# A two-layer graph network on one core: where in a group of matmuls the pieces of layer 1 are run

## The chip, the cores and the metric

The kernel runs on one core of a Trainium2 chip. The metric is the device time of one execution in microseconds (us); the time given for a kernel is the median of its runs. The engines are called TensorE (PE in the profile), VectorE (DVE), ScalarE (ACT), GpSimd (POOL) and SyncE (SP), which issues most DMAs.

## The reference

There are 4096 nodes with 512 features, and a 0/1 adjacency matrix of 4096 x 4096. Layer 0 is graph attention with 8 heads of 64 features, layer 1 is attention inside 32 graphs of 128 nodes. Each is added to its input and normalized by row.

```python
# layer 0
feats = jnp.einsum('nf,hfo->hno', X, W)
dense = s_self[:, :, None] + s_neigh[:, None, :]
dense = jnp.where(dense > 0, dense, 0.2 * dense) * A[None]
out = jnp.einsum('hij,hjo->hio', softmax(dense), feats) + b[:, None, :]
x = layernorm(x + relu(concat_heads(out)))
# layer 1
query, key, value = x @ Wq.T + bq, x @ Wk.T + bk, x @ Wv.T + bv
a = where(same_graph, query @ key.T / sqrt(512), 0.0)
scores = (a + adj + adj) * where(same_graph, 1.0, -1e6)
x = layernorm(x + (softmax(scores) * same_graph) @ value)
```

## The kernel before, in words

**Layer 0** is streamed over the adjacency (`adjacency_streamed_path`). There are four passes, one for each pair of heads (`main_pass(r)`, r = 0 to 3). A pass has four chunks of 1024 target rows (`c` = 0 to 3), and a chunk sums over 32 tiles of 128 source rows. In the last pass they go four at a time, so a chunk has eight groups, numbered 0 to 7 here. For each source tile and head VectorE makes one tile q (L1348, 128 x 1024), and a mark is made of it by ScalarE (L1357), or for every eighth by VectorE (L1353). There are six buffers for q in the last pass, and a group needs eight. TensorE makes three sums: accf, the products of the adjacency with the features f ("A f", L1368, 16 matmuls in a group); acc, the products of the features g with q (L1388, 64 matmuls in the trace); and dens, the products with the marks (L1402), after every second group (the odd ones). After each group ScalarE also checks one or two blocks of the adjacency (L1128, L1129).

**The last pass also carries layer 1.** When a chunk is done, its sums are turned to rows and the rows enter layer 1 in two blocks of 512, called a and b. The work is cut into pieces, which generators run one at a time:

- E (`sums_to_rows`): sums of the chunk that just ended to rows. TensorE transposes into PSUM (L1199, L1222), VectorE reads that (L1202, L1223). E also starts the rows of layer 0 of block a (`rows_of_layer_0`: loads of x and of hp_l on SP's queue, L1144 on VectorE, and the statistics of the normalization, L524 and L525, and L527 and L528 on GpSimd).
- R: the same rows for block b. F: the last part of such a normalization, four operations L532 on VectorE.
- a and b, each in nine steps (`layer_1`, cut by its `yield`s). Steps 1 and 2: each eight transposes L954 and two copies L955 to x1T on ScalarE. Steps 3 and 4: each 16 products L974, to zT by L981 on ScalarE; step 3 has also four L988 on VectorE. Step 5: 32 products L1001 and the softmax (L1010, L1026 and others). Step 6: values of two tiles (2 x 8 products L1046, VectorE's L1054 for each) and between them four transposes L1075. Step 7: the output rows of these two tiles (L1060, L1062, a normalization, the stores). Step 8: values of the two other tiles. Step 9: their output rows.

Block b of a chunk isn't finished in it: its steps 6 to 9 run in the next chunk. So each of chunks 1 to 3 carries a and b of the chunk before it, and chunks 2 and 3 the rest of an older b too; in chunk 1 there is none, and such pieces do nothing.

**What sets the order.** TensorE's instructions run in the order of the program (`tc.manual_schedule(engines={PE})`); the order on the other engines is made by the compiler's planner from program order and the times that it expects. Within a group the program has: the eight q and their marks, accf, two loads of adjacency tiles, the pieces of the *first place* (L1382), acc, the pieces of the *second place* (L1395), dens, the other loads, the checks. `PLAN` and `PLANS` (L1256, L1257) say by letter which pieces go to which place: eight pairs for the eight groups, (first place, second place), the last pair or two different in chunk 3. The PSUM tiles of all pieces come from `misc` (L552), which hands out three banks in turn; so a tile must wait for the readers of the tile three before it. After the last chunk, what is left is run in a fixed order (L1456).

Of the kernel before, what the change touches and what calls it, by code (L numbers as in the profile page):

```python
# [404 lines left out]
def adjacency_streamed_path(  # L405
# [847 lines left out]

    PLAN = [("E", "Fb"), ("b", "b"), ("b", "a"), ("Ra", "Fa"), ("a", "b"), ("ba", "b")]  # L1256
    PLANS = PLAN + [("ab", ""), ("aaba", "")], PLAN + [("a", ""), ("aa", "a")]  # L1257
    plan = {"b": None}

    def run_plan(todo):  # L1260
        for k in todo:
            if k == "F":
                plan[k]()
                continue
            gen = ends[0] if k == "E" else plan[k]
            if gen is not None:
                next(gen)
            if k == "E":
                ends.pop(0)
# [17 lines left out]
    def main_pass(r, ae=None, wide=4):  # L1287

        for c in range(NCH):
# [10 lines left out]
            def pieces(c, group, place):  # L1300
                if r == PR - 1 and c:
                    run_plan(PLANS[c == NCH - 1][group][place])
                elif place == (r == 0):
# [155 lines left out]
@with_exitstack  # L1459
def tile_gat_then_graph_attention(ctx: ExitStack, tc: tile.TileContext, *args: bass.AP):  # L1460
    nc = tc.nc
    keep = ctx.enter_context(tc.tile_pool(name="flag", bufs=1))
    flag = keep.tile([1, 1], I32, name="flag")
    adjacency_streamed_path(tc, flag, *args)
    other = nc.values_load(flag[0:1, 0:1], min_val=0, max_val=1)
    with tc.If(other > 0):
        general_path(tc, *args)
# [42 lines left out]
```

## Time and profile before

| What | us |
|---|---|
| median of 3 runs | 2091.82 |
| lowest and highest of them | 2089.79, 2091.85 |
| the profiled execution, whole | 2089.37 |
| its span in the profile | 2087.0 |
| chunk 1 of the last pass (about) | 158.6 |
| chunk 2 | 172.4 |
| chunk 3 | 162.2 |
| after the last chunk | 120.8 |

The span is read from the trace's start; the chunks of the last pass lie at 1473.0, 1631.6 and 1804.0 us, and the tail starts at 1966.2 us. A line of a page or of waits names engine, tile and line of the code, what it waited for, and then total us, how often and the longest. A line of a timeline has the start, the time taken, engine, line, operation, tiles and how many were merged, and in brackets the idle time before it and what ended that.

### The profile page before, as it was taken

The numbers are of one execution on the slowest core, as the hardware profiler recorded it, in microseconds if no ns is written. First come the engines' busy times: TensorE is split into PE (matmuls) and PEld (weight loads), VectorE is DVE, ScalarE is ACT, GpSimd is POOL, SyncE is SP. The second block draws the span as 40 slices with busy tenths as digits, with TensorE's granted clock in tenths as the row PEclk, the third lists the DMA queues.
The fourth block names the chain that finished last, engine by engine and source line by source line (L and its number), as shares of the span: only waits on it lengthen the run. The fifth ranks groups of instructions, "written<-read, shape, count | busy, mean of one in ns | idle before, by whom it ended". The sixth has DMA issues, their size and how long they took to land. (4 is left out here: it accounts for less than half of the span.)

```text
span 2087.0 us, 38127 instructions
## 1 busy us (share of the span) xinstructions
PE 2055.3 (98%) x15014; PEld 1011.8 (48%) x15014; DVE 1659.8 (80%) x2037; ACT 1537.4 (74%) x1819; POOL 251.0 (12%) x393
## 2 busy tenths in 40 slices
PE   8999999999999999999999999999999999999997
PEld 4556555555545444444445444544454444445443
DVE  5556887888798998797999999998975884886654
ACT  3328898888878899787899899998775666567420
POOL 2343222222100000000000000000300210210111
PEclk9999999999999999999999999999999999999999
DMA  8999999999899999897999899989964773775211
GB/s 253 266 258 242 272 292 257 301 255 298 267 334 331 363 335 342 257 312 254 334 310 339 304 350 329 324 290 360 305 238 145 240 255 126 227 272 165 73 48 43
DMA packets 207881, 551.28 MB, mean 264 GB/s; under 512 B 25292, under 2 KB 66252, under 8 KB 207692
## 3 DMA queue, kind: packets, MB, share of 16 engines
q1 hardware_dynamic: 140748, 425.79, 59.0%
q0 software_dynamic: 62784, 121.91, 23.3%
q8 instruction: 120, 1.97, 0.4%
q10 hardware_dynamic: 4160, 1.05, 0.2%
q14 instruction: 69, 0.57, 0.1%
HBM read 491.79 MB, written 107.22 MB: 287 GB/s over the span
## 5 line engine op out<-in xcount | busy, mean ns | idle before, releaser
L1348 DVE SCALAR_TENSOR_TENSOR q<-p_row,d_all,at 128x1024 f32<-128x1024 f32 x1024 | 1242.5, 1278 | 170.2 <-PE acc L1388 142.0
L1357 ACT ACTIVATE mark<-q,nb_all 128x1024 fp8e4<-128x1024 f32 x896 | 995.8, 1145 | 191.4 <-DVE q L1348 175.3
L1388 PE MATMUL acc<-q,g_s 128*32 128x512 f32 x8192 | 908.3, 594 | 3.2 <-DVE q L1348 2.9
L1388 PEld LDWEIGHTS acc<-q,g_s 128*32 128x32 f32 x8192 | 265.4, 110 | 601.3 <-issue 534.2
L1368 PE MATMUL accf<-at,f_s 128*128 128x512 f32 x2048 | 494.2, 397 | 1.9 <-issue 1.8
L1368 PEld LDWEIGHTS accf<-at,f_s 128*128 128x128 f32 x2048 | 379.8, 189 | 111.0 <-issue 29.1
L1128 ACT ACTIVATE ck<-ck,neg_half_f 128x1024 f32<-128x1024 f32 x128 | 146.0, 1141 | 21.1 <-DMA ck<-in_adj_dram 21.0
L1129 ACT ACTIVATE ck<-ck,neg_quarter 128x1024 f32<-128x1024 f32 x128 | 146.4, 1143 | 1.8
L1113 ACT CAST at<-ps_m 128x1024 fp32r<-128x1024 fp8e4 x128 | 120.2, 1026 | 10.9 <-issue 5.9
L1402 PE MATMUL dens<-mark,e_b 128*6 128x512 fp8e4 x2048 | 124.6, 379 | 0.0
L719 PE MATMUL ps_set<-w_sb_f,xT_f 128*128 128x512 f32 x256 | 116.0, 601 | 0.0
L974 PE MATMUL ps_m<-x1T,M_sb 128*128 128x512 f32 x256 | 113.1, 595 | 1.2 <-ACT x1T L955 1.2
L1046 PE MATMUL ps_m<-wvT,x1T 128*128 128x512 f32 x256 | 114.2, 594 | 0.0
L1233 POOL DMA_DIRECT2D hs_d<-hst x12 | 10.7, 894 | 841.9 <-DVE hst L1223 641.3
L1353 DVE TENSOR_SCALAR mark<-q,d_all 128x1024 fp8e4<-128x1024 f32 x128 | 95.8, 749 | 4.8
L1402 PEld LDWEIGHTS <-e_b 128*6 128x6 bf16 x2048 | 52.5, 86 | 79.4 <-issue 35.3
L1114 POOL DMA_DIRECT2D at_d<-at x128 | 68.7, 537 | 167.8 <-ACT at L1113 108.1
L741 ACT ACTIVATE fst<-fb 128x512 fp32r<-128x512 f32 x32 | 20.4, 637 | 86.1 <-DVE fb L727 52.1
L974 PEld LDWEIGHTS ps_m<-x1T,M_sb 128*128 128x128 f32 x256 | 47.9, 190 | 62.7 <-issue 59.9
L1046 PEld LDWEIGHTS ps_m<-wvT,x1T 128*128 128x128 f32 x256 | 47.6, 190 | 57.2 <-issue 56.0
L719 PEld LDWEIGHTS ps_set<-w_sb_f,xT_f 128*128 128x128 f32 x256 | 48.9, 198 | 49.5 <-issue 49.1
L1054 DVE TENSOR_TENSOR v_t<-ps_m,bv_row 128x512 f32<-128x512 f32 x32 | 21.9, 684 | 62.2 <-PE ps_m L1046 62.2
(177 smaller groups left out, 1136.6 us busy)
## 6 DMA issues: line engine op xcount, KB each, us to landing
at<-at_d SPq DMA_DIRECT2D x384, 512.0 KB, 6.0
ck<-in_adj_dram SPq DMA_DIRECT2D x128, 512.0 KB, 5.4
f_s<-f_d SPq DMA_DIRECT2D x128, 512.0 KB, 7.5
at_d<-at POOLq DMA_DIRECT2D x128, 512.0 KB, 14.7
g_s<-g_d SPq DMA_DIRECT2D x128, 256.0 KB, 5.7
f_d<-fst POOLq DMA_DIRECT2D x32, 512.0 KB, 7.7
p_row<-pu_d SPq DMA_DIRECT2D x32, 512.0 KB, 6.8
a_b<-in_adj_dram POOLq DMA_DIRECT2D x32, 512.0 KB, 16.3
```

Source lines behind the costliest of these rows:

```text
L719: nc.tensor.matmul(pf, tile_j(xTs[k][:, c].rearrange("p u n -> p (u n)"), u), w_sb[:, c, :], start=(c == 0), stop=(c == FC - 1),)
L974: nc.tensor.matmul(pz, L1["M"][:, f, ts(c, P)], x1T[:, f, :], start=(f == 0), stop=(f == FC - 1),)
L1046: nc.tensor.matmul(pv, x1T[:, f, ts(u, P)], L1["wvT"][:, f, :], start=(f == 0), stop=(f == FC - 1),)
L1113: nc.scalar.copy(at, both[:, :, k])
L1128: tc.keep_in_program_order(nc.scalar.activation(ck, ck, AF.Square, bias=neg_half))
L1129: nc.scalar.activation(ck, ck, AF.Abs, bias=neg_quarter, accum_out=binp[:, k : k + 1])
L1348: nc.vector.scalar_tensor_tensor(q, p_row[h], d_j, ats[r, c, j].bitcast(F32), op0=OP.max, op1=OP.mult)
L1353: nc.vector.tensor_scalar(mark, q, d_j, None, op0=OP.is_gt, saturate=False)
L1357: nc.scalar.activation(mark, q, AF.Sigmoid, bias=nb_all[:, j, hh : hh + 1], scale=BIG, saturate=False,)
L1368: nc.tensor.matmul(accf[:, s, :], f_s[j // 4][:, j % 4, w, :], ats[r, c, j][:, ts(s, HB)], start=(j == 0 and w == 0), stop=(j == NT - 1 an ...
L1388: nc.tensor.matmul(acc[o : o + 32, s, :], g_s[j // 4][:, j % 4, h, o % FH : o % FH + 32], qs[j, h][:, ts(s, HB)], start=(j == 0), stop=(j ...
L1402: nc.tensor.matmul(dens[lo : lo + 6, :], e_b[:, j, 2 * r + h, :], marks[j, h][:, ts(s, HB)], start=(j == 0), stop=(j == NT - 1),)
```

## The change

All pieces that stood in the second place of a group are moved to a first place, and the second places are left empty. F moves to the next group; the other pieces stay in their group. Each of a and b keeps the order of its own steps.

```diff
-    PLAN = [("E", "Fb"), ("b", "b"), ("b", "a"), ("Ra", "Fa"), ("a", "b"), ("ba", "b")]
-    PLANS = PLAN + [("ab", ""), ("aaba", "")], PLAN + [("a", ""), ("aa", "a")]
+    PLAN = [("Eb", ""), ("bFb", ""), ("ba", ""), ("Raa", ""), ("Fab", ""), ("bab", "")]
+    PLANS = PLAN + [("ab", ""), ("aaba", "")], PLAN + [("a", ""), ("aaa", "")]
```

Group by group, with the step numbers: group 0 has E and step 6 of the older b ahead of acc (before: step 6 and F behind it); group 1 step 7, F, step 8 (before: F in group 0, and step 8 behind acc); group 2 step 9 and step 1 of a (before: step 1 behind); group 3 R and steps 2 and 3 of a (before: F and step 3 behind); group 4 F, step 4 of a and step 1 of the new b (before: step 1 behind); group 5 step 2 of b, step 5 of a, step 3 of b (before: step 3 behind). Groups 6 and 7 are as before, except in chunk 3, where step 9 of a moves ahead of acc in group 7.

## The prediction

> **What bounds the kernel now.** I read the page first, for which engine is full; then the busy time by chunk of the last pass, because the change acts only there; then the waits of TensorE in that stretch; and then the timelines of the engines around each step that moves.
>
> ```profile
> PE 2055.3 (98%) x15014; PEld 1011.8 (48%) x15014; DVE 1659.8 (80%) x2037; ACT 1537.4 (74%) x1819; POOL 251.0 (12%) x393
> ```
>
> TensorE is full; the others have room on average. In the table by stretch (TensorE, weight loads, VectorE, ScalarE, GpSimd, granted clock, DMA share, GB/s), these are chunks 2 and 3 of the last pass:
>
> ```profile
> 1631.60:1804.00 172.40, 172.04 (x1033) 82.31 (x1029) 128.21 (x197) 110.17 (x148) 23.06 (x37) 1.00 0.63 211
> 1804.00:1966.20 162.20, 161.84 (x984) 75.42 (x980) 125.72 (x183) 103.31 (x132) 18.26 (x29) 1.00 0.53 178
> ```
>
> TensorE has no hole; VectorE is at about 75%. So a TensorE wait added here is paid in full: nothing later has slack to give it back. Of waits that the profile names on TensorE from 1473 to 1964 us, there are only these:
>
> ```profile
> PE acc L1388 <- DVE q L1348: 2.9, 3, 2.5
> PE ps_m L974 <- ACT x1T L955: 0.5, 1, 0.5
> ```
>
> [...] I also took each run of one line's matmuls from its first start to the start of the next run. Undisturbed, a group's 16 products L1368 take 3.8 us and its 64 products L1388 take 6.9 to 7.0. Four kinds of L1388 runs are longer: 12.0 us in group 1 of chunk 1 (5.1 lost), 8.6 and 8.0 in groups 0 and 1 of chunks 2 and 3 (1.6 and 1.0), and 7.5 to 7.8 in group 3 (0.5, 0.5, 0.8). With 0.3 in one L1368 run of chunks 2 and 3, that is 5.9 us in chunk 1 and 3.4 in each of the others: 12.7 us which waits for VectorE's q cost now. The largest, in TensorE's timeline (start, us):
>
> ```profile
> 1489.52 2.68 PE L1388 MATMUL acc<-q,g_s 128*32 128x512 f32 x16
> 1494.66 7.46 PE L1388 MATMUL acc<-q,g_s 128*32 128x512 f32 x46 [2.46 <-DVE q L1348]
> ```
>
> [...] copies L955 below start when the mark ahead of them ends. [...] here an L974 matmul is shown as 592 ns but the next starts 429 ns later, so I use starts. [...]
>
> **The change part by part.** No arithmetic is added. A step moves from behind a group's L1388 to ahead of it. Between two L1388 runs lie the second place of the one group and the first place of the next, so what moves is filler, from one such gap to the gap before; and what was cut by 7 us of L1388 now stands back to back.
>
> *F of the first block* (four L532, VectorE) goes from group 0 to group 1, behind the eight q of group 1. In chunk 1 VectorE idles 1.26 us for GpSimd's rstd and spends 1.9 on F at 1490.2 to 1493.3, with q 3 to 8 queued behind. Without that, q at 1.2 us each from 1490.2 give q8 at 1497.5 and the run ends at 1498.8, not 1501.5: **-2.7**. F then lies before the q of group 2, of which some five (four are enough) are made by the time they are needed. In chunks 2 and 3 no q waits for F.
>
> *Step 6 of b behind E, group 0 of chunks 2 and 3.* All step tiles take turns in three PSUM banks. E uses three (one L1199, two L1222), so step 6's first values need the bank that VectorE's L1202 reads, and its second values that of the second L1223. TensorE and then VectorE in chunk 2:
>
> ```profile
> 1635.79 1.04 PE L1222 MATMUL ps_m<-ident_f,ys 128*128 128x128 f32 x8
> 1636.76 5.36 PE L1388 MATMUL acc<-q,g_s 128*32 128x512 f32 x48
> 1642.33 3.11 PE L1388 MATMUL acc<-q,g_s 128*32 128x512 f32 x16 [0.22 <-DVE q L1348]
> ```
> ```profile
> 1634.78 3.67 DVE L1348 SCALAR_TENSOR_TENSOR q<-p_row,d_all,at 128x1024 f32<-128x1024 f32 x3
> 1638.37 0.32 DVE L1202 TENSOR_REDUCE parts<-ps_m 128x16 f32<-128x48 f32 x2
> ...
> 1648.39 0.66 DVE L1223 TENSOR_TENSOR hst<-ps_m,rd 128x512 f32<-128x512 f32 x1
> ```
>
> TensorE is ready for step 6 at 1636.76, but L1202 stands behind q until 1638.7: 1.95 us. The first values and the transposes L1075 (3.43 + 0.44) end at 1642.6. The second L1223 stands behind the rows of layer 0. Q7 and q8 leave its way (their buffers are freed by L1388, now later). If VectorE fills its wait for the third hp_l load with it, it ends at 1643.5: 0.9 us. If it stays last, the load (issued 1639.2, 4.2 us on the page of DMAs) lands at 1643.4, 1.3 of L1144, 2.6 of L524/L525 and 0.6 follow: 1648.1, 5.5 us. During this TensorE stands with L1388 queued behind; VectorE, six q full, has nothing else. Against it, the 2.9 lost in groups 0 and 1 goes (1.6 + 0.3 + 1.0; 7 us more filler ahead). Net -0.05 to +4.5, I take the middle: **+2.2 in each of two chunks**.
>
> *Step 8 into group 1* (16 L1046, two L1054): its banks are read by L1054 and L1062 3.4 us ahead: 0. *Step 1 of a behind step 9 of b, group 2*: its second transposes take the bank of step 9's first L1060, emptied 0.75 us after it by L1062, unless q stand ahead: 0 to 2.5, **+0.5 each in chunks 2 and 3**, since VectorE idled there by 3.35 us.
>
> *Step 3 of a right behind step 2, group 3, all three chunks.* L974 reads all of x1T, so it needs ScalarE's two copies L955 of step 2. Now 7 us of L1388 lie between, and ScalarE uses most of them. TensorE, then ScalarE, in chunk 2:
>
> ```profile
> 1692.31 1.04 PE L954 MATMUL ps_m<-ident_f,x1b 128*128 128x128 f32 x8
> 1693.27 7.57 PE L1388 MATMUL acc<-q,g_s 128*32 128x512 f32 x64
> 1700.78 1.55 PE L974 MATMUL ps_m<-x1T,M_sb 128*128 128x512 f32 x3
> ```
> ```profile
> 1692.61 4.26 ACT L1357 ACTIVATE mark<-q,nb_all 128x1024 fp8e4<-128x1024 f32 x4
> 1697.72 1.15 ACT L1357 ACTIVATE mark<-q,nb_all 128x1024 fp8e4<-128x1024 f32 x1 [0.85 <-DVE q L1348]
> 1698.77 1.05 ACT L955 COPY x1T<-ps_m 128x512 f32<-128x512 f32 x2
> ```
>
> The fifth mark shown waits for q7 (its idle time in brackets), which now comes after step 3, so the copies go ahead of it, at 1696.8; step 1's copies (1.0), gone earlier, make it 1695.8, x1T ready at 1696.85, against 1693.27: 3.6 us. Chunk 3 gives the same. In chunk 1 the copies start at 1527.22; without q7's mark and step 1's copies they start at 1525.1 and end at 1526.2, 5.6 after TensorE comes at 1520.65 (one more check of blocks stands ahead there). At the least, copies with an empty queue: 0.95. The losses in group 3's L1388 go (0.5, 0.5, 0.8). **+4.8, +3.1, +3.1.** R stays. The L988 and GpSimd operations of step 3 come earlier with it, all off the path (GpSimd is at 12%).
>
> *Group 4*: F, step 4 of a, step 1 of b. F has 7 us of L974 as cover, b's bank was read by L981 earlier: 0. *Group 5*: step 3 of b stands behind step 2 of b and step 5 of a. Step 5's 32 L1001 (3.7 us) are the only cover for the copies:
>
> ```profile
> 1733.21 3.22 ACT L1357 ACTIVATE mark<-q,nb_all 128x1024 fp8e4<-128x1024 f32 x3
> 1736.33 1.05 ACT L955 COPY x1T<-ps_m 128x512 f32<-128x512 f32 x2
> ```
>
> They end at 1737.4, TensorE is there at 1736.55: 0.83, and 3.0 in chunk 3 (1911.93 against 1908.93); up to 1.0 less, as step 1's copies went earlier: **+0.4, +0.4, +2.0**.
>
> *Group 7 of chunk 3*: step 9 right behind step 8 needs the last L1054: 0.7 and its latency, less 0.9 of cover from the first L1060: **+0.5** (0 to 2.5). Its two stores on SP's queue have no loads of this pass behind them; no other DMA moves.
>
> *Changes of tile form on TensorE*: in odd groups L1388 lasts 6.89 with dens L1402 next but 7.00 with a step next, and L974 7.06 there against 6.96 ahead of L1388. A step gone saves 0.2; nine such: **-1.8** (0.4, 0.6, 0.8).
>
> Sum: chunk 1 -2.7 + 4.8 + 0.4 - 0.4 = +2.1; chunk 2 2.2 + 0.5 + 3.1 + 0.4 - 0.6 = +5.6; chunk 3 2.2 + 0.5 + 3.1 + 2.0 + 0.5 - 0.8 = +7.5; together +15.2. The profiled run took 2089.37 us (span 2087.0, 2.4 around it), so 2104.6 for it; the median of the runs is 2091.82, 2.4 above, so **2107**.
>
> **Rivals.** *Copies at once*: ScalarE's order changes so that L955 precedes the marks. Group 3 costs 3 x 0.95 - 1.8 = 1.1, not 11.0, and group 5 nothing, not 2.8: +2.5, 2094. For it: the marks aren't urgent. Against: in the old order the copies let even q7's mark pass. *Filler pays (faster)*: work ahead of L1388 gives VectorE time for q, so all 12.7 us of q waits and 1.8 go, if each reader empties its bank and copies before TensorE asks: 2077. It decides for this if the copies and L1202 come within about 1 us. Against: the rows above show them 2 to 5 us late. *Every reader last*: group 0 at its upper end (+4.6), group 2 too (+4), one more check or mark ahead of each group 3 copy (+3.3): +27, 2119.
>
> **How the numbers follow.** Forecast 0.55, copies at once 0.20, filler pays 0.08, every reader last 0.17. About 0.2% (4.2 us) is what can be told from no change: below 2087.6 is faster, above 2096.0 slower. Faster 0.08; same 0.12 (most of copies at once); slower 0.80. The range, 2091 to 2121, leaves out filler pays and the tails of the outer cases.
>
> **What would show it.** Right: TensorE waits for ACT x1T L955 ahead of L974 in group 3, 3 to 6 us in each chunk; waits for VectorE L1202 and L1223 ahead of L1046 in group 0; L1388 at 7.0 in groups 0, 1 and 3; group 1 of chunk 1 shorter by 2.7. Wrong: L955 directly behind L954 in ScalarE's timeline, or the second L1223 next to the first.

## The result and the profile after

The changed kernel takes 2108.22 us (median; 2106.4 to 2110.48), the kernel before 2091.02 beside it: a ratio of 1.0082, with an interval of 1.007 to 1.0095. It is slower by 17.2 us.

The page's first part hardly moves: TensorE is still "98%" busy, with 3 us more of busy time in a span 21.6 us longer (this profiled execution took 2110.48 us, the slowest of the four). Busy time doesn't show the loss: matmuls that run slowly count as busy too (from 1706 to 1716 us TensorE is busy for 10.00 us of 10.00 at a granted clock of 0.71).

```profile
PE 2058.2 (98%) x15014; PEld 1017.9 (48%) x15014; DVE 1660.6 (79%) x2037; ACT 1532.1 (73%) x1813; POOL 236.0 (11%) x393
```

The loss is in the last pass. The table by stretch (stretch and length, then TensorE, weight loads, VectorE, ScalarE, GpSimd, granted clock, DMA share, GB/s), chunks 1, 2 and 3:

```profile
1473.70:1635.00 161.30, 156.03 (x987) 75.89 (x985) 114.10 (x170) 108.02 (x155) 21.96 (x29) 0.98 0.65 219
1635.00:1818.60 183.60, 174.21 (x1033) 84.91 (x1029) 128.71 (x197) 109.20 (x146) 18.57 (x37) 0.96 0.60 198
1818.60:1987.20 168.60, 162.17 (x984) 77.38 (x980) 127.88 (x190) 101.28 (x129) 17.30 (x33) 0.99 0.53 179
```

The lengths were 158.6, 172.4 and 162.2. TensorE now has holes (5.3, 9.4 and 6.4 us), and in chunk 2 its granted clock is 0.96. TensorE's largest waits from 1470 to 2000 us, with total, number and longest:

```profile
PE ps_m L974 <- ACT x1T L955: 15.8, 3, 7.4
PE ps_m L1046 <- DVE parts L1202: 4.0, 2, 2.0
PE acc L1388 <- DVE q L1348: 0.7, 1, 0.7
```

The first two are waits that the prediction named (the third that it named, for the second L1223, isn't there), and the wait of acc for q has almost gone from this list (2.9 before). They add up to about 17 us net, but that is not the whole account. I took the start of every run of L1368 as the start of a group and compared group by group, after less before (us):

| | group 0 | 1 | 2 | 3 | 4 | 5 | 6 and 7 | chunk |
|---|---|---|---|---|---|---|---|---|
| chunk 1 | 0.0 | -3.2 | 0.0 | +6.2 | 0.0 | -0.3 | 0.0 | +2.7 |
| chunk 2 | +2.9 | -1.6 | +0.5 | +9.7 | 0.0 | -0.3 | 0.0 | +11.2 |
| chunk 3 | +3.0 | -1.6 | +0.5 | +4.9 | 0.0 | -0.3 | -0.1 | +6.4 |

Group 3 alone costs 20.8 us. This is group 3 of chunk 2 on ScalarE and then on TensorE (start, time, and in brackets the idle time before and what ended it):

```profile
1695.38 4.26 ACT L1357 ACTIVATE mark<-q,nb_all 128x1024 fp8e4<-128x1024 f32 x4
1701.72 1.15 ACT L1128 ACTIVATE ck<-ck,neg_half_f 128x1024 f32<-128x1024 f32 x1 [2.08 <-DMA ck<-in_adj_dram]
1702.78 2.17 ACT L1357 ACTIVATE mark<-q,nb_all 128x1024 fp8e4<-128x1024 f32 x2
1704.86 1.05 ACT L955 COPY x1T<-ps_m 128x512 f32<-128x512 f32 x2
```
```profile
1697.53 1.03 PE L954 MATMUL ps_m<-ident_f,x1b 128*128 128x128 f32 x8
1705.95 9.97 PE L974 MATMUL ps_m<-x1T,M_sb 128*128 128x512 f32 x16 [7.39 <-ACT x1T L955]
```

The transposes are done at 1698.5, but the copies stand behind four marks, a check that itself waits 2.08 us for its load, and two more marks. The six are the marks of all q that the buffers hold. Then the 16 products take 9.9 us from the first start to the next run's (1715.86) where 7.0 is usual. That is no dependency: the granted clock (seventh figure after the stretch's length, ahead of the DMA share) is low in the stretch behind the wait, and whole again later:

```profile
1706.00:1716.00 10.00, 10.00 (x20) 4.14 (x24) 8.64 (x25) 1.77 (x4) 2.49 (x4) 0.71 0.52 163
1716.00:1722.70 6.70, 6.70 (x64) 1.94 (x62) 4.82 (x5) 2.91 (x3) 0.01 (x1) 1.00 0.19 50
```

The trace's record of that clock has it at half for 6.83 us in chunk 1 (from 1520.6), 3.41 and 10.24 us in chunk 2 (1643.4, 1701.5) and 3.41 us in chunk 3 (1885.8). Before, there is one such stretch in these chunks, 3.41 us from 1494.8, in the run of acc that had waited for q.

### The profile page after: what moved, and what is told of

Same layout as the page of the kernel before. It is cut to its first block, busy times and chain, and to the rows that moved or that the text cites. A ratio compares the mean times of both kernels' runs of the same rounds, so it can differ in the third digit from the quotient of the medians.

```text
span 2108.6 us, 38122 instructions
## 1 busy us (share of the span) xinstructions
PE 2058.2 (98%) x15014; PEld 1017.9 (48%) x15014; DVE 1660.6 (79%) x2037; ACT 1532.1 (73%) x1813; POOL 236.0 (11%) x393
## 4 chain that ended last, share of the span: by engine, by line
PE 85%; DMA 5%; DVE 4%; issue 3%; ACT 2%; POOL 1%; SPq 0%; POOLq 0%; DVEq 0%; ACTq 0%
PE acc L1388 38%; PE accf L1368 20%; PE ps_m L974 5%; PE dens L1402 5%; PE ps_m L1046 5%; PE ps_set L719 4%; DMA at_d<-at 2%; DVE q L1348 2%; PE ps_m L1001 1%; ACT mark L1357 1%; PE ps_m L1060 1%; PE ps_m L1109 1%; DMA a_b<-in_adj_dram 1%; DMA xt_f<-in_x_dram 1%; PE ps_m L893 1%
## 5 line engine op out<-in xcount | busy, mean ns | idle before, releaser
L1368 PE MATMUL accf<-at,f_s 128*128 128x512 f32 x2048 | 493.6, 397 | 1.9 <-issue 1.8
L1368 PEld LDWEIGHTS accf<-at,f_s 128*128 128x128 f32 x2048 | 379.9, 189 | 116.2 <-issue 33.6
L974 PE MATMUL ps_m<-x1T,M_sb 128*128 128x512 f32 x256 | 119.4, 622 | 16.6 <-ACT x1T L955 16.6
L1402 PE MATMUL dens<-mark,e_b 128*6 128x512 fp8e4 x2048 | 124.2, 379 | 0.0
L1046 PE MATMUL ps_m<-wvT,x1T 128*128 128x512 f32 x256 | 115.6, 600 | 4.0 <-DVE parts L1202 4.0
L1402 PEld LDWEIGHTS <-e_b 128*6 128x6 bf16 x2048 | 54.2, 86 | 77.4 <-issue 34.2
L974 PEld LDWEIGHTS ps_m<-x1T,M_sb 128*128 128x128 f32 x256 | 50.4, 200 | 77.7 <-issue 65.0
L981 ACT ACTIVATE zT<-ps_m,zb 128x512 f32<-128x512 f32 x32 | 21.9, 684 | 80.2 <-PE ps_m L974 80.2
L1046 PEld LDWEIGHTS ps_m<-wvT,x1T 128*128 128x128 f32 x256 | 48.3, 192 | 60.2 <-issue 58.5
```

The source lines that it names most:

```text
L974: nc.tensor.matmul(pz, L1["M"][:, f, ts(c, P)], x1T[:, f, :], start=(f == 0), stop=(f == FC - 1),)
L1046: nc.tensor.matmul(pv, x1T[:, f, ts(u, P)], L1["wvT"][:, f, :], start=(f == 0), stop=(f == FC - 1),)
L1368: nc.tensor.matmul(accf[:, s, :], f_s[j // 4][:, j % 4, w, :], ats[r, c, j][:, ts(s, HB)], start=(j == 0 and w == 0), stop=(j == NT - 1 an ...
L1402: nc.tensor.matmul(dens[lo : lo + 6, :], e_b[:, j, 2 * r + h, :], marks[j, h][:, ts(s, HB)], start=(j == 0), stop=(j == NT - 1),)
```

## The experiments

All groups below are counted as in the table above, each profile against the profile of before. The times of what runs ahead of chunk 1, whose code doesn't change (but for run 3), differ by up to 4.8 us from those of before, so a step is judged by its groups, and a kernel by its ratio.

**1. The changed kernel, step 3 of a put back.**

```diff
-("Raa", "")
+("Ra", "a")
```

> The changed kernel, with step 3 of a put back behind acc in group 3 of every chunk. If the wait of TensorE for the two copies L955 and the halved clock after it make the loss (theory), the 15.8 us of waits and about 7 us of slow matmuls in group 3 go, less what group 3 gained: about 2089 us, that is 0 to 3 us below before. If the loss is spread over the PSUM banks of all moved pieces (rival), no more than 5 us come back: above 2100 us.

2089.29 us, ratio 0.9987 (0.998 to 0.9994). Group 3 gives -0.7, +0.3 and -0.2 in place of +6.2, +9.7 and +4.9; every other group stays as in the changed kernel, except that group 0 of chunks 2 and 3 loses 0.7 and 0.4 us less (in chunk 2 VectorE waits 1.0 us for hp_l there, in place of 1.7). The place of this one letter is the loss, and the rest of the change together is a small gain.

**2. The kernel before, step 3 of a alone moved.**

```diff
-("Ra", "Fa")
+("Raa", "F")
```

> The kernel before, with step 3 of a alone moved ahead of acc in group 3; F and everything else stay. Theory: it loses as the whole change does, 14 to 22 us: 2105 to 2113 us. Rival (the loss needs the other moves too): under 2098 us.

2111.03 us, ratio 1.009 (1.007 to 1.0109). Group 3 gives +7.4, +7.0 and +5.7, all others 0.0. TensorE's waits in the same stretch:

```profile
PE ps_m L974 <- ACT x1T L955: 15.7, 3, 6.7
PE acc L1388 <- DVE q L1348: 2.9, 3, 2.5
```

So it needs none of the other moves. The wait is 15.7 us here and 15.8 there, though divided otherwise (6.7, 4.5 and 4.5 us, against 4.8, 7.4 and 3.6): the queue on ScalarE differs, the mechanism doesn't.

**3. The changed kernel without the checks in the last pass**, to take things out of ScalarE's queue. Their loads go too.

```diff
+    nc.gpsimd.memset(binp, 0.0)
...
-                for group in range(group_0, group_0 + wide // 4) if r else ():
+                for group in range(group_0, group_0 + wide // 4) if 0 < r < PR - 1 else ():
```

> The changed kernel without the checks of adjacency blocks in the last pass (loads, L1128 and L1129; this part of the computation is left out, the sums of the blocks not looked at are set to zero). If the copies are late because of what stands ahead of them in ScalarE's queue (theory), they come earlier by the checks: waits in group 3 of about 2.7, 3 and 3.6 us in place of 4.9, 7.4 and 3.6, and 2099 to 2103 us. If their lateness is set by VectorE's q, which the marks ahead of them need (rival): waits unchanged within 1 us except for the 2 us that one check waited for its load in chunk 2, and about 2105 us.

2104.40 us, ratio 1.0053 (1.0035 to 1.007). Waits of 2.8, 3.8 and 3.8 us (start to start, less one transpose), where the same measure gave 5.0, 7.6 and 3.8. So chunks 1 and 2 lose what the checks held up, and chunk 3, which had no check ahead of its copies, loses nothing: the queue sets the lateness. The total is above what I expected, because the products behind the waits are as slow as ever (runs of 8.7, 10.0 and 9.7 us).

**4. The changed kernel with the copies of that step on VectorE.**

```diff
-            nc.scalar.copy(x1T[:, :, ts(u, P)], pt)
+            if u >= 2 and blk % 2 == 0 and blk < NT // 4 - 2:
+                nc.vector.tensor_copy(x1T[:, :, ts(u, P)], pt)
+            else:
+                nc.scalar.copy(x1T[:, :, ts(u, P)], pt)
```

> The changed kernel with the two copies to x1T of step 2 of a (group 3, chunks 1 to 3) made by VectorE. If the marks and checks ahead of them in ScalarE's queue make them late (theory), they are now behind the q of VectorE instead, which is one or two q of 1.2 us and 1.3 us for themselves: waits of 2 to 4 us in each chunk in place of 4.9, 7.4 and 3.6, and 2098 to 2104 us. If the PSUM bank or the transposes themselves are late (rival), the waits stay as they are: 2107 us or more.

A miss: 2118.51 us, ratio 1.0126 (1.011 to 1.0141). The waits grew:

```profile
PE ps_m L977 <- DVE mv_f L525: 18.6, 2, 9.3
PE ps_m L977 <- DVE x1T L956: 5.3, 1, 5.3
```

(L977 is L974 here and L956 a copy; L525 is what VectorE ran directly behind the second copy, and the list names it in the copy's place.) I had counted only the q in VectorE's queue. The rows that R starts come ahead too: in chunk 2 the second copy starts at 1709.7, 8.5 us after the transposes end, behind L1144 (with 1.0 us of waiting for hp_l) and the statistics. The wait follows the queue of whichever engine holds the copies; a bank or the transposes as the cause don't fit, since they are the same in all three kernels.

**5. The changed kernel with work in the wait**: products of finished tiles, into a PSUM tile of which one column is copied and not used.

```diff
+        if blk % 2 == 0 and blk < NT // 4 - 2:
+            pz = misc([P, 4 * P])
+            for f in range(FC):
+                nc.tensor.matmul(
+                    pz, L1["M"][:, f, :P], L1["wvT"][:, f, :], start=(f == 0), stop=(f == FC - 1)
+                )
+            nc.vector.tensor_copy(small.tile([P, 1], F32, name="spare"), pz[:, :1])
```

> The changed kernel with added work that nobody uses: four products of 128x512 (8 matmuls of 0.43 us, 3.4 us) in front of step 3 of a in group 3 of each chunk, where TensorE waits 4.9, 7.4 and 3.6 us. If the matmuls after a long wait run at half the clock because of the wait (theory), the clock stays whole in two or three of the chunks and the kernel gets faster in spite of 10 us of added work: 2101 to 2105 us, with L974 runs of 7.0 instead of 8.7 to 9.9. If the slow L974 have another reason, such as a late zT or PSUM bank (rival): 2108 or more, the L974 runs as long as before.

2108.61 us (2106.39 to 2112.72), ratio 1.0082 (1.006 to 1.0105): the time of the changed kernel, so the gain that I expected didn't come. The clock did what was expected in two of the three chunks. Chunk 1, where L985 is L974:

```profile
1518.90 3.60 PE L974 MATMUL ps_m<-wvT,M_sb 128*128 128x512 f32 x8
1524.29 7.11 PE L985 MATMUL ps_m<-x1T,M_sb 128*128 128x512 f32 x16 [1.79 <-ACT x1T L955]
```

The filler shortens the wait from 4.8 to 1.8 us, and the products behind it take 7.0 us in place of 9.2. In chunk 3 they take 7.1 (8.7), in chunk 2, where 3 us of wait are left, still 8.7 (9.9). Group 3 sums to 17.9 us in place of 20.8; in chunk 3 the gain is lost again, as acc waits for q (1.2 us). So the slow products went with the wait: with 1.8 us of it left in chunk 1 and 0.2 in chunk 3 they took 7.0 and 7.1 us, with 3.0 left in chunk 2 they took 8.7. That a filler pays is not shown.

**6. Steps 3 and 6 put back**, all else as in the changed kernel.

```diff
-("Eb", "") ... ("Raa", "")
+("E", "b") ... ("Ra", "a")
```

> The changed kernel with step 3 of a back behind acc (group 3) and step 6 of b back behind acc (group 0). In the trace step 6 behind E cost 2.9 us in group 0 and gained 1.6 in group 1, in each of two chunks. Theory: 2 to 3 us below the kernel with step 3 alone put back, near 2086 us. Rival (the filler ahead of acc in group 0 is worth more than the wait for L1202): slower than that one by 1 to 3 us.

2082.12 us, ratio 0.9962 (0.995 to 0.9975), and again 2083.20, 0.9965 (0.9951 to 0.9978), beside run 9:

> The kernel with steps 3 and 6 put back once more, beside the one with step 1 put back too: 2082 us, ratio to before 0.995 to 0.997.

Groups 0 and 1 of chunks 2 and 3 give 0.0 and -1.3. Against run 1 (+2.2 and +2.6; -1.6), step 6 behind E costs 1.9 and 2.3 us a chunk. No stretch of halved clock is left in the three chunks (granted clock 1.00 in each). This kernel beats both, by 0.4% the one before.

**7. F alone moved**, from the kernel before.

```diff
-("E", "Fb"), ("b", "b")
+("E", "b"), ("bF", "b")
```

> The kernel before with F of the first block alone moved to group 1, behind step 7. Theory: the run of acc in group 1 of chunk 1 is 3 us shorter (1.7 of it because the clock is not halved) and nothing else changes: 2088 us, 0.1 to 0.2% faster than before. Rival (the q of group 2 then come late by the 1.9 us of F): no difference.

2085.36 us, ratio 0.9973 (0.9965 to 0.998): group 1 gives -3.2, -1.0 and -1.0, the rest of the chunks 0.2 or less. TensorE in chunk 1, acc of group 1:

```profile
1490.80 9.42 PE L1388 MATMUL acc<-q,g_s 128*32 128x512 f32 x62
```

One run of 62, without a hole, and 8.8 us from its start to that of L1402 (before, 12.0 us with a hole of 2.46). The 3.2 us are F's 1.9 and the 1.26 that VectorE idled for rstd; in the kernel before, the last products of this run start at 1500.63, 0.05 us after q8 is made, so VectorE's q set its end, not the clock as I had thought. F is more than half of what run 6 gains.

**8. Step 2 of a one group earlier**, so that all pieces stay behind A f and yet acc lies between steps 2 and 3.

```diff
-("ba", ""), ("Raa", "")
+("baa", ""), ("Ra", "")
```

> The changed kernel with step 2 of a moved on one group forward, to group 2, so that all pieces are still behind A f but 7 us of acc lie between step 2 and step 3. Theory (only the missing distance between L954 and L974 costs): no wait for L955 in group 3, 2087 to 2090 us. Rival (the two places differ by themselves): above 2095 us.

2094.30 us, ratio 1.002 (1.0012 to 1.0027): not what I expected. The wait for L955 ahead of L974 is gone, but there are others:

```profile
PE ps_m L1046 <- DVE parts L1202: 4.0, 2, 2.0
PE acc L1388 <- DVE q L1348: 4.0, 3, 2.4
...
PE ps_m L954 <- ACT x1T L955: 1.4, 2, 1.1
PE ps_m L954 <- DVE y_f L1062: 0.5, 1, 0.5
```

Group 2 gives +1.3, +2.2 and +2.2 (16 transposes in a row ask for four banks of three), and group 3 -1.8, +0.9 and +2.2. In chunk 2, q7 of group 3 is made only at 1707.8, 5 us after acc began: the rows of R, L988 and part of F went ahead. So the distance between the steps was not all; what VectorE is given between two runs of acc counts as well. And with step 6 of b ahead of E in group 0 besides:

```diff
-("Eb", "")
+("bE", "")
```

> As the one with step 2 in group 2, and in group 0 step 6 of b goes ahead of E, so that its products don't ask for the banks that E's readers hold. Theory: the 2 us waits for L1202 in chunks 2 and 3 go and group 0 gets the filler: 3 to 5 us less than that one, near 2084 us. Rival (E is late for the rows of layer 0, and F or step 1 then waits for them): no gain, or 2 to 6 us more than that one.

2092.00 us, ratio 1.0 (0.9991 to 1.0009), 2.3 us less than the one above, as expected in sign, but less than I thought. The waits for L1202 are gone, but E, now behind step 6, has its own for L1054 (2.6 us in chunks 2 and 3 together; group 0 of chunk 2 still gives +2.6), and group 2 now gives up to +5.4, with 4.1 us of waits of L954 for L955. The rival had foreseen a late E; most of the named waits are for the copies of step 1.

**9. Step 1 of a put back too**, from run 6.

```diff
-("ba", "")
+("b", "a")
```

> The kernel with steps 3 and 6 put back, and step 1 of a (group 2) put back behind acc as well. In the profiles the moved step 1 costs 0.5 us in each of chunks 2 and 3, because acc then waits for q. Theory: 1 us less than that kernel, about 2081 us; a rival in which step 1 is free either way gives the same. The difference is near what can be told apart.

2084.73 us, ratio 0.9968 (0.9957 to 0.9979), beside 2083.20: no difference that can be told. In the groups it gains 0.5 in group 2 of chunks 2 and 3 and loses 0.2 to 0.9 in group 3: where step 1 lies makes no difference that these runs show.

## Why the prediction was right, and where only its sum was

The forecast of 2107 us and the direction hold, by the mechanism forecast: TensorE waits for the copies L955, since the acc between steps 2 and 3 is gone, and for L1202 behind E. Runs 1 and 2 show the first by removal and alone, runs 3 and 4 that the queue ahead of the copies sets it. The profiles put 20.3 us into the three chunks, the prediction 15.2; the medians differ by 17.2 (the profiled pair lies further apart, 2110.48 and 2089.37). The terms, though, were less good than the sum, and one of the prediction's own signs of being wrong, "the second L1223 next to the first", did come.

- **Group 3** was mis-sized: +11.0 predicted, +20.8 measured (20.1 alone, run 2). The waits were put at 5.6, 3.6 and 3.6 us and are 4.8, 7.4 and 3.6. In chunk 2 the queue held a check that waited for its own load (3.1 us with the wait), which a trace of before couldn't show; it was the "one more check" of the rival "every reader last". The term that I left out is the clock: the products behind the waits took 2.2, 2.9 and 1.7 us longer. So of the 9.8 us too little, 3.0 are waits and 6.8 clock.
- **F** was right in chunk 1 (-2.7 predicted, -3.2 measured; run 7). "In chunks 2 and 3 no q waits for F" failed: it is -1.0 in each. The 1.0 us that acc lost there in group 1, which I gave to a lack of filler, was F's, with its 1.26 us wait for rstd in VectorE's queue (run 7).
- **Step 6 behind E** was right in size, by terms that partly cancel: +2.2 a chunk predicted, 1.9 and 2.3 by run 1 against run 6. The wait for L1202 is 2.0 (1.95 predicted). The wait for the second L1223 isn't there: VectorE, with no q to make, ran it right behind the first, the lower end of my bounds. In chunk 2:

```profile
1641.77 0.31 DVE L1202 TENSOR_REDUCE parts<-ps_m 128x16 f32<-128x48 f32 x2
...
1643.79 1.29 DVE L1223 TENSOR_TENSOR hst<-ps_m,rd 128x512 f32<-128x512 f32 x2
...
1647.41 0.56 DVE L1144 SCALAR_TENSOR_TENSOR x1b<-hp_l,x1b 128x384 f32<-128x384 f32 x1 [1.73 <-DMA hp_l<-hs_d]
```

  What came short is the gain of 1.6 us that was set against it. With the filler ahead, acc of group 0 was to take 7.0 us; it takes 7.3 in chunk 2 and 9.1 in chunk 3. The slow chain that I had put behind L1223 (the load of hp_l, L1144, L524) stands in VectorE's queue ahead of q7 and q8. In chunk 3, where acc starts at 1833.30:

```profile
1837.08 1.00 DVE L532 TENSOR_SCALAR x1b<-x1b,mv_f,rstd_f 128x512 f32<-128x512 f32 x2 [0.91 <-POOL rstd_f L528]
1838.00 3.67 DVE L1348 SCALAR_TENSOR_TENSOR q<-p_row,d_all,at 128x1024 f32<-128x1024 f32 x3
```
```profile
1839.33 3.11 PE L1388 MATMUL acc<-q,g_s 128*32 128x512 f32 x16 [0.67 <-DVE q L1348]
```

  The first products of q7 and of q8 start 0.05 us after each is made, so the 2.1 us above 7.0 are q, although the wait that the profile names is 0.67. In chunk 2 TensorE came to acc later, since the clock was at half and the first eight L1046 took 5.2 us and not 3.4, but acc there ends by q8 too: the two chunks lose the same, 2.9 and 3.0 us.
- **Group 5** failed: +2.8 predicted with nothing for the tile form, 0 measured. The 3.6 us of L1001 cover the copies: in chunk 3 they end at 1929.7, and L974 follows at 1930.3. I had moved only step 1's copies off the queue of before; but between the start of A f and these copies in chunk 3 one operation of a check now stands where there were four.
- **Group 2** came out at +0.5 as said, but as acc waiting for q, not as a bank, and run 9 shows it is given back in group 3. **Group 4** 0 as said. **Group 7** of chunk 3: -0.1 against +0.3 with the tile form, nothing to wait for.
- **Changes of tile form** are seen in group 5 as -0.3 (0.2 said). In groups 1 and 3 they can't be parted from the rest.

So the hit on the sum owes something to errors that cancel: about 10 us too little in group 3, against some 2.5 too little gain from F and 3.5 us of loss in groups 5 and 7 that didn't come. That part is luck. Of the rivals, "filler pays" holds in one place only: the named waits of acc for q fell from 2.9 to 0.7. But run 7 shows that most of that gain is F, which isn't filler. Not settled is whether any filler in group 3 pays: run 5 gains 2.9 us there by the groups, and nothing by the medians.

## What to carry to other kernels

Two steps that depend on one another through another engine need work between them on the full engine, and the amount is set by what stands in that other engine's queue at that place (TensorE waited 3.6 to 7.4 us here for two copies of 0.5), not by the time of the copy. Moving filler into a gap takes it out of the neighbouring one; list for each gap what every engine has to do in it before moving anything. A small operation that waits on a slow helper (F, for rstd) belongs behind the urgent work of its engine: here that one letter was worth 0.27%.

## What the runs showed of the hardware that I had not expected

A wait of TensorE cost more than its length here. With the waits of 4.8, 7.4 and 3.6 us in group 3 of the changed kernel's three chunks the granted clock was at half for 6.83, 10.24 and 3.41 us (in part still within the wait), and products that start 0.43 us apart at whole clock came 0.85 to 1.0 us apart; the 16 products behind the waits lost 2.2, 2.9 and 1.7 us.

The length of a wait alone doesn't say what follows. In group 0 of the changed kernel TensorE waits 2.0 us in chunk 2 and 2.0 us in chunk 3. In chunk 2 the granted clock was at half for 3.41 us, from 1.2 us after the wait; in chunk 3 it stayed at 1.00 from 1820 to 1842 us. And near 957 us the traces of both kernels have 6.83 us at half clock with no idle time of TensorE just before them, where it had run products of a single column (L912 and L928, 128x1). What decides when such a stretch starts and how long it lasts is not shown by these runs.

Half clock showed no cost where acc had to wait for VectorE's q in any case. In group 0 of chunk 2, with 3.41 us of half clock, the first eight L1046 took 5.2 us (3.5 in chunk 3), and the group lost 2.9 us; that of chunk 3, at whole clock, lost 3.0. In group 1 of chunk 1 of the kernel before a part of acc ran in 3.41 us at half clock, and its last products still started 0.05 us after q8 was made.
